# The first steps of a linear attention in an order written by hand on three engines

## The chip, the cores and the metric

The kernel runs on one core of a Trainium2 chip. The metric is the time on the device in microseconds (us), the median of several executions. A core has five engines that each work through an instruction stream of their own: TensorE (PE, the matmuls), VectorE (DVE), ScalarE (ACT), GpSimd (POOL) and SyncE (SP, here the issuer of plain transfers). They wait for one another by semaphores.

## The reference

Four images go through a small vision tower: a tokenizer, a first layer (attention over the images, then a mixture of six experts, two for each token), and a second layer (a linear attention, then four experts and a shared MLP). Only the join of the two layers and the linear attention matter here:

```
h   = h + combined                              # the two experts' rows of each token, weighted
x   = layernorm(h)
q, k, v = split(x @ W_qkv + b_qkv)
q, k = q - mean(q), k - mean(k)
q2, k2 = q*q, k*k
k2 = l2norm_over_tokens(k2 / (sum(k2) + 1e-7))  # a norm for each channel, over all tokens of the image
q2 = l2norm_over_channels(q2 / (sum(q2) + 1e-7))
kv = einsum('bnc,bnd->bcd', k2, v)
h   = h + (v + q2 @ kv / sqrt(N)) @ W_out + b_out
```

## The kernel before

**Tiles and units.** An image has 784 distinct tokens in seven tiles of 112 tokens. The linear attention works on *units* of four or three tiles: units 0 and 1 are image 0, units 2 and 3 are image 1, and so on up to unit 7. The residual stream `h` stays on chip.

**From the experts to the units.** The first layer's experts work in 30 blocks of 256 rows and write their rows to `yrows` in DRAM. When the last block is written, the rows of a unit come back by indirect gathers: `fetch(u)` (from L1352, the gather in L1361) has POOL issue two of them for each tile (one for each of a token's two experts) into a tile `ys`. Eight gathers make a unit of four tiles, six one of three. The pool of `ys` has three buffers (`bufs=3`), so a later unit's gathers wait until an earlier unit's rows have been read.

**Statistics.** `stats_one(u, j)` (from L1369) is DVE work on one tile: two multiply-adds `h += ys * wk` (L1375), one for each gathered row, each of which has to wait for its gather; then the layernorm's statistics (L1384, L1385). `normalise(u)` takes the root on ACT (L1394), the reciprocal (L1395) and writes the normalised rows `xa` (L1398); then `residual(u)` adds a bias row to `h` (L1409).

**Attention.** For each unit: `x_t` turns `xa` on PE; `q_k` (L1566 to L1575) makes q and k in PSUM (`pqk`), DVE adds the bias (L1570), ACT squares with running sums; `scales` (L1589 to L1603) makes the scale of each token and applies it on both engines, and squares the scaled k into `sq`; `fold` (L1610 to L1615) sums `sq` over the tiles on DVE; `q_t` turns q. For each image: `k_x` (from L1622) sums the squares over tokens on PE (`pn`), takes the norm `kn` (L1632 to L1634), multiplies k by x on PE (`pukx`, L1640) and scales the result into `g` (L1644). `g_t` turns `g`, `kv_out` multiplies it by `Wvo` and DVE finishes `kvo` (L1670), and `rows_out` (L1681, L1686) multiplies x and q into the output and adds it to `h` (L1692). `layer1_weights` makes `Wvo` and `bvo` once, from the weights.

**Who sets the order.** Some stretches of the program stand inside `tc.manual_schedule(engines=...)`: on the engines listed, their instructions keep the written order among themselves. Everything else is placed by a scheduler, which may also put it between the instructions of a hand-written stretch: in the program before, the two copies that make `bvs` in `layer1_weights` stand far ahead, between the first layer's attention steps. In the kernel before, the block loop of the experts is by hand on DVE and SP, and it also holds the statistics of units 0 and 1; all of the linear attention is left to the scheduler.

The loop of the linear attention goes over steps `u`. Step 0 fetches unit 3, turns unit 1 and makes `q_k`, `scales` and `fold` of unit 0; step 1 does the same for unit 1, with the weights in between. In step 1 `q_k` also makes the statistics of unit 2, tile by tile:

```
            if u:
                stats_one(u + 1, j)
```

Of the kernel before, what the change touches and what calls it, by code (L numbers as in the profile page):

```python
# [21 lines left out]
F32 = mybir.dt.float32  # L22
# [5 lines left out]
P = 128  # L28
TT = 112
NI = 4  # L30
TPI = 7
# [4 lines left out]
D = 256  # L36
# [24 lines left out]
def tile_vit_tower(ctx: ExitStack, tc: tile.TileContext, a: dict, out: bass.AP):  # L61
# [112 lines left out]
    def col(key, i=0, n=P):  # L174
        return cols[:n, rows[key] + i : rows[key] + i + 1]
# [415 lines left out]
        )  # L591

    def layer1_weights():
        WvT = w1p.tile([P, 2, D], F32, tag="WvT", name="WvT")
        pt = ps_tile("pwv").rearrange("p (k i) -> p k i", k=2)
        for k in range(2):
            for c in range(2):
                nc.tensor.transpose(
                    pt[:, k, c * P : (c + 1) * P],
                    Wqkv[:, c, 2 * D + k * P : 2 * D + (k + 1) * P], ident,  # L600
                )
        nc.vector.tensor_copy(WvT, pt)
        Wvo = w1p.tile([P, 2, D], F32, tag="Wvo", name="Wvo")
        for c in range(2):
            pw = ps_tile("pwvo")[:, :D]
            for k in range(2):
                nc.tensor.matmul(
                    pw, WvT[:, k, c * P : (c + 1) * P], Wout[:, k, :],
                    start=(k == 0), stop=(k == 1),
                )  # L610
            nc.scalar.copy(Wvo[:, c, :], pw)
        bvs = w1p.tile([P, 2, P], F32, tag="bvs", name="bvs")
        for k in range(2):
            nc.vector.tensor_copy(bvs[:, k, :], col("bv", k).to_broadcast([P, P]))
        bvo = w1p.tile([P, D], F32, tag="bvo", name="bvo")
        pw = ps_tile("pbvo")[:, :D]
        for k in range(2):
            nc.tensor.matmul(pw, bvs[:, k, :], Wout[:, k, :], start=(k == 0), stop=(k == 1))
        nc.vector.tensor_copy(bvo, pw)
        bres = bout  # L620
        nc.vector.tensor_tensor(bres, bout, bvo[:TT], ALU.add)
        return Wvo, bvo, bres

# [800 lines left out]
    with tc.manual_schedule(engines={mybir.EngineType.DVE, mybir.EngineType.SP}):  # L1426
        own_weights(NEARLY)
        turned(NEARLY)
        for i in range(NEARLY, NBLK + 1):
            if i < NBLK:  # L1430
                load(i + 3)
                hidden(i, 0)
            rows_back(i - 1)
            own_weights(i + 1)
            turned(i + 1)
            if i < NBLK:
                hidden(i, 1)
            if i == NEARLY + 1:
                centred_weights()
            for u in range(3):  # L1440
                if i - 1 == after[u]:
                    fetch(u)

            for u, wait, two in ((0, 4, 1), (1, 2, 2)):
                j = (i - 1 - after[u] - wait) * two
                for k in range(j, j + two):
                    if 0 <= k < units[u][2]:
                        stats_one(u, k)
                    elif k == units[u][2]:
                        normalise(u)  # L1450
            if i - 1 == after[0] + 10:
                x_t(0)
    layer0.close()


# [94 lines left out]
    def q_k(u, j0, j1):  # L1550

        n = units[u][2]
        xT = xTs[u]
        if j0 == 0:
            qks[u] = lin.tile([TT, GT, 2 * D], F32, tag="qk", name="qk")
            sumsof[u] = (
                small.tile([TT, GT, 2], F32, tag="ss", name="ss"),
                small.tile([TT, GT], F32, tag="s4", name="s4"),
            )
        qk = qks[u]  # L1560
        ss, s4 = sumsof[u]
        junk = lin.tile([TT, D], F32, tag="junk", name="junk", bufs=1)
        for j in range(j0, min(j1, n)):
            pqk = ps_tile("pqk")[:TT]
            for c in range(2):
                nc.tensor.matmul(  # L1566
                    pqk, xT[:, c, cut(j, 1)], Wqkv[:, c, : 2 * D],
                    start=(c == 0), stop=(c == 1),
                )
            nc.vector.tensor_tensor(qk[:, j, :], pqk, bqkv[:, : 2 * D], ALU.add)  # L1570

            for i in range(2):
                half = qk[:, j, i * D : (i + 1) * D]
                nc.scalar.activation(half, half, AF.Square, accum_out=ss[:, j, i : i + 1])  # L1574
            nc.scalar.activation(junk, qk[:, j, :D], AF.Square, accum_out=s4[:, j : j + 1])  # L1575
            if u:
                stats_one(u + 1, j)
        if j1 >= n and u:
            if u + 1 < len(units) and units[u + 1][2] > n:
                stats_one(u + 1, n)  # L1580
            normalise(u + 1)

    def scales(u):

        b, j0, n = units[u]
        qk = qks[u]
        ss, s4 = sumsof.pop(u)

        nc.vector.tensor_scalar(ss[:, :n], ss[:, :n], 1e-7, None, ALU.add)  # L1589
        nc.scalar.activation(s4[:, :n], s4[:, :n], AF.Sqrt, bias=zero[:TT])  # L1590
        nc.vector.scalar_tensor_tensor(
            ss[:, :n, 0], ss[:, :n, 0], 1e-12, s4[:, :n], ALU.mult, ALU.max
        )
        nc.vector.reciprocal(ss[:, :n], ss[:, :n])
        uk = uks[u] = lin.tile([TT, GT, D], F32, tag="uk", name="uk", bufs=3)
        sq = lin.tile([TT, GT, D], F32, tag="sq", name="sq", bufs=1)
        for j in range(n):
            nc.scalar.activation(uk[:, j, :], qk[:, j, D:], AF.Copy, scale=ss[:, j, 1:2])
            nc.vector.tensor_scalar(
                qk[:, j, :D], qk[:, j, :D], ss[:, j, 0:1], None, ALU.mult  # L1600
            )
        for j in range(n):
            nc.scalar.activation(sq[:, j, :], uk[:, j, :], AF.Square)  # L1603
        return sq

    def fold(u, sq):
        b, j0, n = units[u]
        if j0 == 0:
            acc = sums[b] = lin.tile([TT, 2, D], F32, tag="acc", name="acc")
            nc.vector.tensor_tensor(acc, sq[:, 0:2, :], sq[:, 2:4, :], ALU.add)  # L1610
        else:
            acc = sums[b]
            nc.vector.tensor_tensor(acc, acc, sq[:, 0:2, :], ALU.add)
            nc.vector.tensor_tensor(acc[:, 0, :], acc[:, 0, :], sq[:, 2, :], ALU.add)
            nc.vector.tensor_tensor(acc[:, 0, :], acc[:, 0, :], acc[:, 1, :], ALU.add)  # L1615
# [5 lines left out]

    def k_x(b):  # L1622

        acc = sums.pop(b)
        pn = psum_s.tile([P, 512], F32, tag="pss", name="pn")
        for c in range(2):
# [6 lines left out]
        nc.vector.tensor_scalar(kn, kn, 1e-12, None, ALU.max)  # L1633
        nc.vector.reciprocal(kn, kn)  # L1634
        g = gs[b] = lin.tile([P, 2, D + 2], F32, tag="g", name="g")
        for c in range(2):
            pg = ps_tile("pukx")[:, : D + 2]
            for j in range(TPI):
                u, k = (2 * b, j) if j < GT else (2 * b + 1, j - GT)
                nc.tensor.matmul(  # L1640
                    pg, uks[u][:, k, c * P : (c + 1) * P], xas[u % 4][:, k, : D + 2],
                    start=(j == 0), stop=(j == TPI - 1),
                )
            nc.vector.tensor_scalar(  # L1644
                g[:, c, :], pg, kn[:, c : c + 1], REP / math.sqrt(REP * SEQ),
                ALU.mult, ALU.mult,
            )
# [45 lines left out]

    squares = {}
    for u in range(len(units) + 2):
        b, odd = divmod(u - 2, 2)
        one_image = u >= 2 and not odd
        if u == 0:  # L1700
            fetch(3)
            x_t(1)
            q_k(0, 0, GT)
            squares[0] = scales(0)
            fold(0, squares.pop(0))
            continue
        if u < len(units):
            fetch(u + 3)
        if u == len(units):
            shared = shared1(0)  # L1710
        if one_image:
            k_x(b)
            q_t(u - 1)
        if u == 2:
            gT = g_t(0)
            kv_out(0, gT)
            rows_out(0)
            x_t(2)
        if u < len(units):
            q_k(u, 0, 2)  # L1720
        if one_image and b:
            gT = g_t(b)
        if u < len(units):
            q_k(u, 2, GT)
            if u == 1:
                lw.extend(layer1_weights())
                Wvo, bvo = lw[:2]
            squares[u] = scales(u)
        if one_image and b:
            kv_out(b, gT)  # L1730
        if u == len(units) - 1:
            rows_in(0)
            turn_rows(0)
            gate(0)
        if 2 <= u < len(units) - 1:
            x_t(u + 1)
        if u == 3:
            for k in range(3):
                residual(k)
        if u >= 2 and (b or odd):  # L1740
            rows_out(u - 2)
        if u < len(units):
            fold(u, squares.pop(u))
            if u % 2:
                q_t(u - 1)
    linear.close()
# [94 lines left out]
```

## Time and profile before

| | before |
|---|---|
| time, median of 3 | 816.67 us (815.66 to 820.11) |
| span of the profiled execution | 814.5 us |
| PE busy | 736.9 us, 90% of the span |
| DVE busy | 514.7 us, 63% |
| ACT busy | 318.5 us, 39% |
| POOL busy | 131.9 us, 16% |

The shares are means over stages that are limited by different things. The linear attention runs from about 506 us to 669 us, and the change lies in its first forty. For that stretch one needs the busy time of each engine in slices of ten microseconds, the timeline of DVE and POOL, and the chain of waits.

### The profile page before, as it was taken

How to read it: one execution, taken by the hardware profiler on the slowest of the kernel's cores; microseconds unless marked ns; L12 is line 12 of the kernel's file. 1: busy time of each engine (PE TensorE's matmuls, PEld its weight loads, DVE VectorE, ACT ScalarE, POOL GpSimd, SP SyncE). 2: the span in 40 equal slices, each digit the busy share in tenths (PEclk: the TensorE clock that was granted, in tenths of full speed). 3: DMA queues.
4: the chain of work that ended last, by engine and by line, in shares of the span. 5: the costliest groups of instructions: out<-in, count | busy, mean ns of one | idle time of the engine just before them, and what ended most of it. 6: DMA issues, size and time to landing. Idle time of an engine off the chain costs nothing. (4 is left out here: it accounts for less than half of the span.)

```text
span 814.5 us, 11185 instructions
## 1 busy us (share of the span) xinstructions
PE 736.9 (90%) x3669; PEld 520.4 (64%) x3669; DVE 514.7 (63%) x1619; ACT 318.5 (39%) x758; POOL 131.9 (16%) x151
## 2 busy tenths in 40 slices
PE   1879998899788887989999999699999999999996
PEld 1757785555555655878888887375776675555553
DVE  4477897486767985535545756699984745554441
ACT  0424434555376475333223322627544503222221
POOL 4200000000006450750013020676000000000000
PEclk9999999999999988999999999899999999999999
DMA  8999991000002167433234234322000002233323
GB/s 193 341 425 425 420 421 65 1 0 1 0 1 62 40 230 231 142 118 113 91 98 141 81 113 123 90 88 73 2 1 1 0 16 69 84 102 94 93 86 114
DMA packets 59182, 97.52 MB, mean 120 GB/s; under 512 B 15486, under 2 KB 49460, under 8 KB 54260
## 3 DMA queue, kind: packets, MB, share of 16 engines
q1 hardware_dynamic: 52700, 81.47, 28.7%
q0 software_dynamic: 6224, 14.13, 6.0%
q10 hardware_dynamic: 200, 1.21, 0.7%
q8 instruction: 29, 0.48, 0.2%
q14 instruction: 29, 0.24, 0.1%
HBM read 31.04 MB, written 65.74 MB: 119 GB/s over the span
## 5 line engine op out<-in xcount | busy, mean ns | idle before, releaser
L901 POOL DMA_INDIRECT xrows<-xn,pos x56 | 60.2, 1074 | 274.0 <-ACT kq L665 233.1
L1361 POOL DMA_INDIRECT ys<-yrows,pos x56 | 56.6, 1011 | 146.7 <-DMA yrows<-yb 130.6
L1168 PE MATMUL pb<-xTb,own 128*128 128x256 f32 x240 | 59.4, 392 | 3.8 <-DVE r L764 1.6
L1174 ACT ACTIVATE hb<-pb,own 128x256 f32<-128x256 f32 x74 | 35.0, 473 | 61.1 <-PE pb L1168 52.7
L1168 PE MATMUL pb<-hb,own 128*128 128x256 f32 x240 | 58.2, 385 | 0.3 <-DVE hb L1176 0.3
L1185 PE MATMUL pyb<-own,hb 128*128 128x256 f32 x240 | 56.9, 379 | 0.2 <-ACT hb L1174 0.2
L1168 PEld LDWEIGHTS pb<-xTb,own 128*128 128x128 f32 x240 | 45.4, 197 | 12.9 <-ACT hb L1174 1.9
L297 PE MATMUL pt<-ident,xn 112*128 112x112 f32 x280 | 42.3, 282 | 12.2 <-DVE xn L482 6.9
L1566 PE MATMUL pqk<-Wqkv,lxT 128*112 128x512 f32 x112 | 49.7, 594 | 0.5 <-ACT lxT L81 0.5
L1185 PEld LDWEIGHTS pyb<-own,hb 128*128 128x128 f32 x240 | 45.4, 190 | 6.8 <-ACT hb L1174 0.6
L297 PEld LDWEIGHTS pt<-ident,xn 112*128 112x128 f32 x280 | 32.6, 149 | 26.2 <-ACT xn L778 9.2
L1191 DVE TENSOR_TENSOR yb<-pyb,eb 128x512 f32<-128x512 f32 x30 | 20.7, 690 | 44.9 <-PE pyb L1185 44.5
L1168 PEld LDWEIGHTS pb<-hb,own 128*128 128x128 f32 x240 | 43.8, 192 | 6.2 <-DVE hb L1176 0.9
L306 PE MATMUL pe<-xT,eW 128*128 128x448 f32 x112 | 45.2, 546 | 0.0
L1158 ACT COPY xTb<-ptb 128x512 f32<-128x512 f32 x30 | 17.5, 583 | 62.7 <-PE ptb L1154 62.7
L1176 DVE TENSOR_SCALAR hb<-pb,own 128x256 f32<-128x256 f32 x46 | 22.1, 481 | 29.5 <-PE pb L1168 29.5
L317 PE MATMUL pwo<-Wo,oT 128*112 128x256 f32 x112 | 29.0, 412 | 7.5 <-DVE oT L730 6.7
L1566 PEld LDWEIGHTS pqk<-Wqkv,lxT 128*112 128x112 f32 x112 | 19.3, 177 | 24.8 <-issue 23.0
L690 DVE SCALAR_TENSOR_TENSOR prod<-kq 128x784 f32<-128x784 f32 x32 | 30.3, 969 | 7.3 <-ACT kq L665 5.0
L1574 ACT ACTIVATE qk<-qk 112x256 f32<-112x256 f32 x56 | 22.8, 407 | 28.5 <-DVE qk L1570 28.3
L306 PEld LDWEIGHTS pe<-xT,eW 128*128 128x128 f32 x112 | 20.2, 190 | 20.9 <-issue 20.7
L1145 DVE COPY own<-ew 128x1540 f32 x30 | 28.8, 963 | 3.9 <-DMA Wout<-in_L_attn_W_out_dram 1.1
(339 smaller groups left out, 1519.1 us busy)
## 6 DMA issues: line engine op xcount, KB each, us to landing
xrows<-nothing SPq DMA_DIRECT2D x19, 1024.0 KB
yrows<-nothing SPq DMA_DIRECT2D x19, 1024.0 KB
out_dram<-h SPq DMA_DIRECT2D x84, 112.0 KB
xb<-xrows SPq DMA_DIRECT2D x30, 256.0 KB
yrows<-yb SPq DMA_DIRECT2D x30, 256.0 KB
ew<-in_L_ffn_expert_w_dram SPq DMA_DIRECT2D x6, 768.0 KB
wb<-wd SPq DMA_DIRECT2D x28, 112.0 KB
img<-in_x_dram ACTq DMA_DIRECT2D x2, 588.0 KB
```

Of the source, the lines that this page charges most:

```text
L297: nc.tensor.transpose(pt[:, j * TT : (j + 1) * TT], xn[:, j, c * P : (c + 1) * P], ident[:TT, :TT])
L306: nc.tensor.matmul(pm[: wcols.stop - wcols.start, :n], w[:, c, wcols], xT(c), start=(c == 0), stop=(c == chunks - 1),)
L317: nc.tensor.matmul(pm[:, i, :], xT(c, t), w[:, c, :], start=(c == 0), stop=(c == chunks - 1))
L690: nc.vector.scalar_tensor_tensor(prod, qTs[s][:, o, :], 1.0, kT[:, o, t * SEQ : (t + 1) * SEQ], ALU.mult, ALU.mult, accum_out=atts[s][:, o ...
L901: put = nc.gpsimd.indirect_dma_start(out=xrows[:, :], out_offset=bass.IndirectOffsetOnAxis(ap=pos[:, k, t0 + j : t0 + j + 1], axis=0), in_ ...
L1145: nc.vector.tensor_copy(w, ewf[0][:, bass.ds(off, EW)])
L1168: nc.tensor.matmul(pm, wm[:, c, o * P : (o + 1) * P], src[:, c, :], start=(c == 0), stop=(c == 1),)
L1174: nc.scalar.activation(dst[:, o, :], pm, AF.Relu, bias=b)
L1185: nc.tensor.matmul(pm[:, t, :], src[:, c, t * P : (t + 1) * P], wm[:, c, :], start=(c == 0), stop=(c == 1),)
L1361: got = nc.gpsimd.indirect_dma_start(out=y[:, j, k, :], out_offset=None, in_=yrows[:, :], in_offset=bass.IndirectOffsetOnAxis(ap=pos[:, k, ...
L1566: nc.tensor.matmul(pqk, xT[:, c, cut(j, 1)], Wqkv[:, c, : 2 * D], start=(c == 0), stop=(c == 1),)
L1574: nc.scalar.activation(half, half, AF.Square, accum_out=ss[:, j, i : i + 1])
```

## The change

The first two steps of the loop are taken out of it and written out in a fixed order on DVE, PE and ACT: both units' `q_k` and `scales` first, then the folding of their squares, with unit 2's statistics tile by tile between the later steps. `fetch(3)` and `fetch(4)` now stand ahead of that stretch; before, `fetch(4)` stood in step 1. For this to be written, some functions are cut in two or moved:

- `scales` leaves the squares to a new `squares`, called later.
- `k_x` makes its products first and keeps both PSUM tiles; the norm of the sums moves to a new `k_norm`, for all images.
- `layer1_weights` is a generator in three pieces, and its `bvs` copies move ahead.
- `q_k` makes the next unit's statistics from unit 2 on, instead of unit 1.
- `x_t(1)` moves to the end of the block loop, and the bias of units 0 and 1 only (not 2) is added in step 3.

The aim is that the scales of two units, and with them k and q, are ready early, and that the third unit's statistics stand behind them.

```diff
@@ block loop
+            if i == NBLK:
+                x_t(1)
@@ q_k
-            if u:
+            if u > 1:
                 stats_one(u + 1, j)
-        if j1 >= n and u:
+        if j1 >= n and u > 1:
...
             normalise(u + 1)
@@ scales
-        for j in range(n):
-            nc.scalar.activation(sq[:, j, :], uk[:, j, :], AF.Square)
-        return sq
+    def squares(u):
+        sq = sqs[u] = lin.tile([TT, GT, D], F32, tag="sq", name="sq", bufs=1)
+        for j in range(units[u][2]):
+            nc.scalar.activation(sq[:, j, :], uks[u][:, j, :], AF.Square)
@@ k_x: products first, the norm of the sums in k_norm
...
@@ the loop's first two steps
-    squares = {}
-    for u in range(len(units) + 2):
...
-        if u == 0:
-            fetch(3)
-            x_t(1)
-            q_k(0, 0, GT)
-            squares[0] = scales(0)
-            fold(0, squares.pop(0))
-            continue
+    pgs = {}
+    fetch(3)
+    fetch(4)
+    with tc.manual_schedule(engines=by_hand):
+        q_k(0, 0, GT)
+        q_k(1, 0, 2)
+        scales(0)
+        weights = layer1_weights()
+        q_k(1, 2, GT)
+        next(weights)
+        scales(1)
+        next(weights)
+        q_t(0)
+        squares(0)
+        fold(0)
+        squares(1)
+        stats_one(2, 0)
+        stats_one(2, 1)
+        next(weights)
+        fold(1)
+        k_x(0)
+        stats_one(2, 2)
+        k_norm(0)
+        q_t(1)
+        stats_one(2, 3)
+        Wvo, bvo = lw[:2]
+        gT = g_t(0)
+        normalise(2)
+        kv_out(0, gT)
+        rows_out(0)
+        x_t(2)
+    for u in range(2, len(units) + 2):
```

More of the change, by code (lines that the diff above doesn't have):

```diff
@@ L602, in layer1_weights @@
         nc.vector.tensor_copy(WvT, pt)
+        bvs = w1p.tile([P, 2, P], F32, tag="bvs", name="bvs")
+        for k in range(2):
+            nc.vector.tensor_copy(bvs[:, k, :], col("bv", k).to_broadcast([P, P]))
+        yield
         Wvo = w1p.tile([P, 2, D], F32, tag="Wvo", name="Wvo")
@@ L611, in layer1_weights @@
             nc.scalar.copy(Wvo[:, c, :], pw)
[L612 to L615, printed above, removed]
         pw = ps_tile("pbvo")[:, :D]
@@ L618, in layer1_weights @@
             nc.tensor.matmul(pw, bvs[:, k, :], Wout[:, k, :], start=(k == 0), stop=(k == 1))
+        yield
+        bvo = w1p.tile([P, D], F32, tag="bvo", name="bvo")
         nc.vector.tensor_copy(bvo, pw)
@@ L621, in layer1_weights @@
         nc.vector.tensor_tensor(bres, bout, bvo[:TT], ALU.add)
-        return Wvo, bvo, bres
+        lw.extend((Wvo, bvo, bres))
+        yield
     scale = REP / math.sqrt(CHEAD) / math.sqrt(REP * SEQ)
@@ L1595, in scales @@
         uk = uks[u] = lin.tile([TT, GT, D], F32, tag="uk", name="uk", bufs=3)
-        sq = lin.tile([TT, GT, D], F32, tag="sq", name="sq", bufs=1)
         for j in range(n):
@@ L1601, in scales, with fold @@
             )
-        for j in range(n):
-            nc.scalar.activation(sq[:, j, :], uk[:, j, :], AF.Square)
-        return sq
-    def fold(u, sq):
+    def squares(u):
+        sq = sqs[u] = lin.tile([TT, GT, D], F32, tag="sq", name="sq", bufs=1)
+        for j in range(units[u][2]):
+            nc.scalar.activation(sq[:, j, :], uks[u][:, j, :], AF.Square)
+    sqs = {}
+    def fold(u):
+        sq = sqs.pop(u)
         b, j0, n = units[u]
@@ L1622, in k_x, with k_norm @@
     def k_x(b):
+        pgs[b] = []
+        for c in range(2):
+            pg = ps_tile("pukx")[:, : D + 2]
+            for j in range(TPI):
+                u, k = (2 * b, j) if j < GT else (2 * b + 1, j - GT)
+                nc.tensor.matmul(
+                    pg, uks[u][:, k, c * P : (c + 1) * P], xas[u % 4][:, k, : D + 2],
+                    start=(j == 0), stop=(j == TPI - 1),
+                )
+            pgs[b].append(pg)
+    def k_norm(b):
         acc = sums.pop(b)
@@ L1635, in k_x @@
         g = gs[b] = lin.tile([P, 2, D + 2], F32, tag="g", name="g")
[L1636 to L1643, printed above, removed]
+        for c, pg in enumerate(pgs.pop(b)):
             nc.vector.tensor_scalar(
@@ L1692, in rows_out @@
             nc.vector.tensor_tensor(ht, pm[:, : len(two), :], ht, ALU.add)
-    squares = {}
-    for u in range(len(units) + 2):
-        b, odd = divmod(u - 2, 2)
-        one_image = u >= 2 and not odd
-        if u == 0:
-            fetch(3)
-            x_t(1)
-            q_k(0, 0, GT)
-            squares[0] = scales(0)
-            fold(0, squares.pop(0))
-            continue
+    pgs = {}
[30 more added lines that the diff above has]
+    for u in range(2, len(units) + 2):
+        b, odd = divmod(u - 2, 2)
+        one_image = not odd
         if u < len(units):
@@ L1710, in tile_vit_tower @@
             shared = shared1(0)
-        if one_image:
+        if one_image and b:
             k_x(b)
+            k_norm(b)
             q_t(u - 1)
[L1714 to L1718, printed above, removed]
         if u < len(units):
@@ L1724, in tile_vit_tower @@
             q_k(u, 2, GT)
[L1725 to L1728, printed above, removed]
+            scales(u)
+            squares(u)
         if one_image and b:
@@ L1734, in tile_vit_tower @@
             gate(0)
-        if 2 <= u < len(units) - 1:
+        if u < len(units) - 1:
             x_t(u + 1)
         if u == 3:
-            for k in range(3):
+            for k in range(2):
                 residual(k)
-        if u >= 2 and (b or odd):
+        if b or odd:
             rows_out(u - 2)
         if u < len(units):
-            fold(u, squares.pop(u))
+            fold(u)
             if u % 2:
```

## The prediction

> **What bounds the kernel now.** I read the busy time in slices of 10 us first, to find which engine limits which part of the linear attention:
>
> ```profile
> 510.00:520.00 10.00, 9.04 (x25) 3.72 (x23) 5.50 (x14) 4.75 (x22) 6.83 (x8) 1.00 0.24 70
> 520.00:530.00 10.00, 4.40 (x10) 3.53 (x11) 8.56 (x27) 7.59 (x30) 7.56 (x9) 0.69 0.31 93
> ...
> 560.00:570.00 10.00, 10.00 (x44) 6.71 (x43) 9.96 (x33) 8.23 (x32) 4.24 (x5) 1.00 0.22 64
> 570.00:580.00 10.00, 10.00 (x51) 7.70 (x50) 9.73 (x30) 3.01 (x9) 0.00 (x0) 1.00 0.01 2
> ```
>
> The columns are the slice, then PE, PEld, DVE, ACT and POOL busy, the clock that PE was granted, and DMA. PE idles 5.6 us in 520 to 530, with its clock down to 0.69 for part of it. From 550 on it never rests: 89.5 of 90 us to 640. So PE bounds everything after 550, and a delay of PE before that cannot be won back. The chain of waits shows how PE enters that stretch:
>
> ```profile
> 538.63 0.89 DVE g L1644 x2
> ...
> 540.78 1.99 PE pkvo L1666 x8
> ...
> 543.64 0.86 PE pout L1686 x4
> ```
>
> DVE finishes `g` of image 0 at 539.5, PE makes `pkvo`, DVE makes `kvo`, and at 543.64 PE starts the first product with `kvo` (L1686). This is the clock I use: when does this product start in the changed program?
>
> The timelines of DVE and POOL show what DVE waits for early on:
>
> ```profile
> 513.67 0.48 DVE L1375 SCALAR_TENSOR_TENSOR h<-ys,wk,h 112x256 f32<-112x256 f32 x1 [2.92 <-DMA ys<-yrows,pos]
> 514.07 0.68 DVE L1570 TENSOR_TENSOR qk<-pqk,bqkv 112x512 f32<-112x512 f32 x1
> ```
> ```profile
> 511.04 0.92 POOL L1361 DMA_INDIRECT ys<-yrows,pos  x1 [21.73 <-DMA yrows<-yb]
> 512.26 0.93 POOL L1361 DMA_INDIRECT ys<-yrows,pos  x1 [0.30 <-issue]
> ...
> 520.87 0.99 POOL L1361 DMA_INDIRECT ys<-yrows,pos  x1 [0.30 <-DVE h L1375]
> ...
> 528.70 0.92 POOL L1361 DMA_INDIRECT ys<-yrows,pos  x1 [0.30 <-DVE xa L1398]
> ...
> 538.73 0.92 POOL L1361 DMA_INDIRECT ys<-yrows,pos  x1 [0.30 <-DVE xa L1398]
> ...
> 546.81 0.92 POOL L1361 DMA_INDIRECT ys<-yrows,pos  x1 [0.30 <-issue]
> ...
> 552.22 1.37 POOL L1361 DMA_INDIRECT ys<-yrows,pos  x1 [0.30 <-issue]
> ```
>
> POOL issues the gathers of units 2 to 7 without a rest from 511.04, about 1.23 us apart: unit 2 (eight), unit 3 from 520.87 (six), unit 4 from 528.70 (eight), unit 5 from 538.73, unit 6 from 546.81; 552.22 is the fifth of unit 6. The view of the tile `ys` gives the landing after the issue:
>
> ```profile
> DMA to landing us min/median/max: 2.6/2.7/3.3
> ```
>
> And DVE obeys its order. PE made `pqk` tiles every 1.74 us (12.18 us for seven), the third by about 511.7; its addition ran at 514.07, because a multiply-add that waited 2.92 us for a gather stood ahead of it.
>
> [...]the gathers here take 0.92 to 1.44 us, so the pace has a floor of 1.23 us and may stretch. [...]here `pwvo` (eight matmuls) took 3.78 us after 6.56 us idle, against 1.99 us for `pkvo`, equally large.
>
> **The change part by part.** PE's order stays up to `pukx`; ACT's and DVE's do not. The decisive part does not stand in the diff but in the order of the changed program's DVE instructions. Unit 2's statistics are now fixed behind `fold(0)`. The statistics of units 3 to 6 are outside the block, and the scheduler has put their multiply-adds *into* it, each with its wait for its gather, ahead of what the block was written for. In order, with units read from the operands:
>
> ```
> qk unit 0 (4), qk unit 1 tile 0
> ys unit 3: three; qk unit 1 tile 1; ys unit 3: three
> ys unit 4: two, and between them the scales of unit 0; ys unit 4: one
> qk unit 1 tile 2, WvT, bvs; ys unit 4: four, and between them the scales of unit 1
> ys unit 4: one; ys unit 5: six; ys unit 6: one; lqT; ys unit 6: two; fold(0)
> ys unit 2 (landed) and ys unit 6 (fourth, fifth), in turn
> statistics of units 2 to 6, bvo, fold(1), residual(1); kn, g; ...; kvo
> ```
>
> So before `g` DVE waits for the fifth gather of unit 6, the 33rd of the train. Before, what stood ahead of `g` needed only gathers issued by about 535. The new wait's queue holds unit 1's q and k, both units' scales, `WvT` (for which PE waits), `fold` (for which `pn` waits), `g` and `kvo`.
>
> *The wait.* Gather 33 was issued at 552.22. At the floor it would be 511.04 + 32 x 1.227 = 550.3; POOL's buffers come free in time either way (unit 5 now takes unit 3's, whose last gather lands about 530). With 2.7 us to land: 553.0 to 555.5; I take 554.0[...]. Up to there each gather comes 1.2 us after the last and DVE has less than that to do between, so the arrival sets the time. The matmuls behind `WvT` (about 537) and the scales of unit 1 (about 540) are done long before.
>
> *From there to the end of `g`* (spacing from start to start in DVE's timeline): 5 multiply-adds x 0.39 = 1.95; 14 statistics x 0.33 = 4.6; 10 aggregates x 0.09 = 0.9; `bvo` and `bres` 0.7; `fold(1)` 0.60 + 0.33 + 0.33 = 1.26; residual(1) 0.84; `kn` twice 0.3; `g` twice 0.79. Sum 11.3 us. `pn` and `kn`'s root fit inside: the sums are complete at 6.8 us, the root took 1.3 us after them before, and `kn` is due at 9.6.
>
> *From `g` to the end of `kvo`:* `lqT` 0.41, 5 multiply-adds 1.95, 3 statistics 1.0, aggregate 0.1, 3 reciprocals 0.36, 5 `xa` x 0.31 = 1.55, residual(2) 1.12, `kvo` 0.8: 7.3 us. PE needs 3.3 us from `g` to the end of `pkvo` (539.5 to 542.8)[...]: hidden beside this.
>
> So `kvo` ends at 554.0 + 11.3 + 7.3 = 572.6, where it ended at 543.30: L1686 starts **29.0 us** later than at 543.64.
>
> *The clock.* PE will have idled from about 550 in pieces. `pwvo` and `pbvo` lost 2.45 us to the low clock before (3.57 + 1.57 from start to start, against 1.83 + 0.86). The output products lose between 0 and 2.5; I take 1.2.
>
> *Later images.* The norm now follows the products. For images 1 and 2, 3.4 us of `pqk` hide it. For the last, only `lqT`'s transposes (0.57) and `pws` (0.1) stand between, against some 1.6 us from `pn` to the end of `g` (root 0.26, `kn` 0.35, `g` 0.87, hops): 0.9 us.
>
> *What it saves.* The 7 us of PE idle before `pwvo` lie in front of the same wait and are worth nothing. DVE will be lighter after 573, since units 3 to 6 have been added already, but PE is full there: nothing. The split of `scales`, the moved `bvs`, `x_t(1)` and the residual move hidden work: nothing.
>
> Sum: 29.0 + 1.2 + 0.9 = 31.1, so 816.67 + 31.1 = 847.8, rounded to **848 us**.
>
> **The rivals.** *(a) The hoisted waits are cheap.* The written order then does what it is for, PE's idle before `pwvo` shrinks, and 816.7 - 7 = about 810 us. For it: DVE had 4.5 of 10 us free in 510 to 520. Against: POOL's gathers are issued at a fixed pace, and DVE let `qk` wait for one. Slower is missed only if the stream is not run as built; the trace of before follows its own built order exactly. *(b) About the same:* the delay is taken up later. Against it: PE is busy 89.5 of 90 us after 550. 817 us. *(c) A smaller delay:* gathers at the floor, DVE's run of small instructions faster (18.6 us becomes 15) and no clock loss: 816.7 + 553.0 - 554.0 + 29.0 - 3.6 + 0.9 = 842 us or a little under. *(d) A larger one:* [...](1.44 us for each gather would put the 33rd 5 us later) and the full clock loss: 848 + 5 + 1.3 + some waits after `kvo` (unit 6's and 7's last multiply-adds stand there too) = 854 to 858 us.
>
> **How the numbers follow.** The forecast (843 to 852) 0.70; (c) 0.11; (d) 0.13; (a) 0.04; (b) 0.02. The range takes in most of (c) and (d): 839 to 855. Faster by over 0.5% 0.04, within 0.5% 0.02, slower 0.94.
>
> **What would show it.** Right: DVE waits for gathers 15 to 20 times between 520 and 557, with waits of about 1 us; the fifth multiply-add of unit 6 near 554; `g` near 565, `kvo` near 572; PE busy under half of 520 to 570, and full after. POOL's train keeps its pace. Wrong: `g` before 550, or PE resting after 575, or the gathers themselves moving.

## The result and the profile after

The changed kernel takes **845.24 us** (843.52 to 848.91) beside 818.72 us (815.66 to 821.21) for the kernel before, measured together: ratio 1.0332, 95% interval 1.0297 to 1.0367, so 3.3% slower. The forecast was 848, the range 839 to 855. In the two profiles the span grew from 814.5 to 842.7 us, by 28.2 us.

The busy time in slices of 10 us, with the columns of the prediction (slice; PE, PEld, DVE, ACT, POOL busy; clock granted to PE; DMA):

```profile
510.00:520.00 10.00, 9.43 (x25) 3.86 (x23) 2.76 (x4) 5.99 (x28) 7.04 (x8) 1.00 0.26 74
520.00:530.00 10.00, 0.00 (x0) 0.00 (x0) 3.51 (x8) 1.49 (x7) 7.56 (x9) 0.71 0.33 96
...
550.00:560.00 10.00, 0.25 (x2) 0.25 (x2) 9.25 (x31) 1.03 (x3) 7.58 (x8) 0.58 0.30 86
560.00:570.00 10.00, 7.48 (x26) 5.49 (x26) 10.00 (x33) 1.96 (x6) 2.44 (x3) 0.57 0.15 43
...
580.00:590.00 10.00, 9.76 (x28) 4.29 (x27) 9.73 (x31) 7.09 (x31) 0.00 (x0) 1.00 0.00 0
```

PE does nothing at all from 520 to 530, where it was busy for 4.40 us before, and 0.25 us from 550 to 560, where it was busy for 9.52. From 580 on it is all but full again (9.76). What was lost was lost between 520 and 571.

DVE's timeline has the multiply-adds of `h`, `g` and `kvo` (the start, the duration of the group, what it waited for in brackets); POOL's has the first gather of the train and the last ahead of `g`; the view of the tile `ys` sums up who waited for it (us, times):

```profile
523.33 0.48 DVE L1379 SCALAR_TENSOR_TENSOR h<-ys,wk,h 112x256 f32<-112x256 f32 x1 [7.04 <-DMA ys<-yrows,pos]
...
553.02 0.48 DVE L1379 SCALAR_TENSOR_TENSOR h<-ys,wk,h 112x256 f32<-112x256 f32 x1 [0.19 <-DMA ys<-yrows,pos]
...
563.18 0.86 DVE L1660 TENSOR_SCALAR g<-pukx,kn 128x258 f32<-128x258 f32 x2
...
570.35 0.86 DVE L1686 SCALAR_TENSOR_TENSOR kvo<-bvo,g,pkvo 128x256 f32<-128x256 f32 x2
```
```profile
510.82 0.92 POOL L1365 DMA_INDIRECT ys<-yrows,pos  x1 [21.12 <-DMA yrows<-yb]
...
550.29 0.92 POOL L1365 DMA_INDIRECT ys<-yrows,pos  x1 [0.30 <-issue]
```
```profile
  DVE h L1379: 19.2, 18
...
DMA to landing us min/median/max: 2.6/2.7/3.9
```

POOL's second line here is the 33rd gather, issued at 550.29: 32 steps of 1.23 us after the first. It lands 2.7 us later, and at 553.02 the multiply-add that waited for it starts. `g` ends at 564.04 and `kvo` at 571.21. In all, DVE's multiply-adds waited 18 times, 19.2 us. The first wait, 7.04 us, is the longest: it is for unit 3's first gather, the ninth of the train. Unit 2's eight go ahead of it on POOL, but DVE adds them only after 550. The chain that ended last now runs through DVE where it ran through PE's `pkvo` before:

```profile
570.43 0.40 DVE kvo L1686
...
570.88 1.12 PE pout L1702 x4
```

And PE, whose waits name what it needed each time, first in the kernel before, then in the changed one:

```profile
525.60 3.78 PE L607 MATMUL pwvo<-Wout,WvT 128*128 128x256 f32 x8 [6.56 <-DVE WvT L602]
...
543.48 1.03 PE L1686 MATMUL pout<-kvo,lqT 128*112 128x256 f32 x4
```
```profile
536.01 3.78 PE L612 MATMUL pwvo<-Wout,WvT 128*128 128x256 f32 x8 [16.58 <-DVE WvT L603]
...
559.75 1.02 PE L1650 MATMUL pn<-ones,acc 112*128 112x1 f32 x4 [11.41 <-DVE acc L1625]
...
570.88 1.12 PE L1702 MATMUL pout<-kvo,lqT 128*112 128x256 f32 x4 [0.92 <-DVE kvo L1686]
```

It waited 16.58 us for `WvT` (6.56 before), 11.41 for the sums `acc`, and 0.92 for `kvo`. The product with `kvo` starts at 570.88 instead of 543.48. (The chain of waits puts the start in the kernel before at 543.64; from here on the timeline's 543.48 is used.)

### The profile page after: what moved, and what is told of

The parts are those of the page before. It is cut to its first block, busy times and chain, and to the rows that moved or that the text cites. A ratio compares the mean times of both kernels' runs of the same rounds, so it can differ in the third digit from the quotient of the medians.

```text
span 842.7 us, 11182 instructions
## 1 busy us (share of the span) xinstructions
PE 740.4 (88%) x3669; PEld 522.7 (62%) x3669; DVE 516.8 (61%) x1619; ACT 319.1 (38%) x758; POOL 129.5 (15%) x151
## 3 DMA queue, kind: packets, MB, share of 16 engines
q1 hardware_dynamic: 52700, 81.47, 28.2%
## 5 line engine op out<-in xcount | busy, mean ns | idle before, releaser
L1365 POOL DMA_INDIRECT ys<-yrows,pos x56 | 54.4, 972 | 146.1 <-DMA yrows<-yb 130.0
L1172 PE MATMUL pb<-hb,own 128*128 128x256 f32 x240 | 58.1, 385 | 0.3 <-DVE hb L1180 0.3
L1379 DVE SCALAR_TENSOR_TENSOR h<-ys,wk,h 112x256 f32<-112x256 f32 x56 | 26.2, 475 | 19.4 <-DMA ys<-yrows,pos 19.2
L1580 ACT ACTIVATE qk<-qk 112x256 f32<-112x256 f32 x56 | 22.8, 408 | 33.7 <-DVE qk L1576 33.7
```

The costliest lines, as they stand in the source:

```text
L1172: nc.tensor.matmul(pm, wm[:, c, o * P : (o + 1) * P], src[:, c, :], start=(c == 0), stop=(c == 1),)
L1365: got = nc.gpsimd.indirect_dma_start(out=y[:, j, k, :], out_offset=None, in_=yrows[:, :], in_offset=bass.IndirectOffsetOnAxis(ap=pos[:, k, ...
L1379: nc.vector.scalar_tensor_tensor(h[:, t, :], ys[u][:, j, k, :], wk[:, k, t : t + 1], h[:, t, :], ALU.mult, ALU.add,)
```

## The experiments

The forecast came out, but that does not prove its reasons. **Theory A**: the scheduler put the multiply-adds of units 3 to 6 into DVE's hand-written stretch, each with its wait for a gather, and what the stretch is for had to wait behind them. The rivals say that the time went elsewhere: to the hand-written order on PE and ACT, to the norms that now follow the products, or to the amount of DVE's work in the stretch.

Two numbers are read from each profile: **lead**, from the start of the first `pqk` product to the start of the first output product with `kvo`, and **tail**, from there to the end of the span.

| kernel | start of pqk | product with kvo | lead | tail | span | median (ratio to before, interval) |
|---|---|---|---|---|---|---|
| before | 506.42 | 543.48 | 37.1 | 271.0 | 814.5 | 818.72 |
| changed | 506.81 | 570.88 | 64.1 | 271.8 | 842.7 | 845.24 (1.0332, 1.0297 to 1.0367) |
| units 3 and up barred | 510.11 | 547.64 | 37.5 | 283.9 | 831.5 | 833.45 (1.0202, 1.0153 to 1.0251) |
| units 4 and up barred | 509.09 | 560.44 | 51.4 | 281.4 | 841.8 | 842.12 (1.0314, 1.026 to 1.0369) |
| units 5 and up barred | 506.31 | 561.54 | 55.2 | 271.7 | 833.2 | 836.8 (1.0272, 1.0218 to 1.0325) |
| before, norm after the products | 509.48 | 548.52 | 39.0 | 273.2 | 821.7 | 821.93 (1.0058, 1.0038 to 1.0079) |
| changed, DVE free | 506.06 | 548.17 | 42.1 | 273.4 | 821.6 | 824.3 (1.0095, 1.0068 to 1.0122) |
| before, WvT early | 507.44 | 545.25 | 37.8 | 271.0 | 816.2 | 817.57 (0.9998, 0.9973 to 1.0023) |

The start of `pqk` differs by up to 4 us between the profiles, and by 3.1 us even between the kernel before and the one with the norm after the products, whose code is the same up to there. So leads, tails and places counted from the first `pqk` are compared, and not places in the span.

Six more runs, in two jobs, stand apart. The kernel before took about 5% longer there (854.16 and 859.06 us), and the profiles of all six show long waits that nothing in the program releases, so their numbers are not compared with those of the table.

### Bars ahead of the later units

In three kernels the multiply-adds of the later units read a copy of the gather weights `wk` which DVE makes as the last step of the hand-written stretch. They cannot be placed before it. With N = 2, 3, 4 the bar holds units 3, 4 or 5 and all above:

```
+    wks = [wk]
-                h[:, t, :], ys[u][:, j, k, :], wk[:, k, t : t + 1], h[:, t, :],
+                h[:, t, :], ys[u][:, j, k, :], wks[u > N][:, k, t : t + 1], h[:, t, :],
...
         x_t(2)
+        wk2 = lina.tile([TT, 2, NT], F32, tag="wk2", name="wk2", bufs=1)
+        nc.vector.tensor_copy(wk2, wk)
+        wks.append(wk2)
```

All of units 3 and up barred:

> The changed kernel, but the multiply-adds of units 3 to 7 read a copy of the weights that DVE makes at the end of the hand-written stretch, so the scheduler cannot put them inside it. Theory (waits for hoisted gathers): DVE waits for no gather of unit 3 or later before kvo; the first product with kvo (L1686 of the kernel before) starts near 540 us instead of 570.9, and the time is 812 to 818 us. Rival A (the written order itself is slow: two units' scales and the weights ahead of everything): still 838 us or more. Rival B (the norm after the products, in all images, costs most of it): still 838 us or more.

Measured 833.45 us: the time is a miss, and the product starts at 547.64 instead of near 540. Of the span, 3.3 us more than in the changed kernel lie ahead of `pqk`. PE's timeline:

```profile
525.89 1.99 PE L612 MATMUL pwvo<-Wout,WvT 128*128 128x256 f32 x8 [3.17 <-DVE WvT L603]
...
547.64 1.29 PE L1703 MATMUL pout<-kvo,lqT 128*112 128x256 f32 x4
...
565.91 1.42 PE L297 MATMUL pt<-ident,xa 112*128 112x112 f32 x6 [3.66 <-DVE xa L1403]
...
578.36 0.42 PE L297 MATMUL pt<-ident,xa 112*128 112x112 f32 x2 [3.22 <-DVE xa L1403]
```

PE waits 3.17 us for `WvT` instead of 16.58, and the lead is back to 37.5 us, 0.4 more than in the kernel before. So it was the later units' work in the stretch that made it 64.1. But the tail grew by 12.1 us over the changed kernel's: two new waits for `xa`, 3.66 and 3.22 us, and a low clock behind them (0.76 and 0.84 from 560 to 580). The statistics of units 3 and 4 now all come after the stretch, and POOL's timeline shows what else they hold:

```profile
562.11 0.92 POOL L1365 DMA_INDIRECT ys<-yrows,pos  x1 [11.65 <-DVE h L1380]
```

The tile `ys` has three buffers. Until unit 3's rows are read, unit 6's gathers cannot start: POOL rests 11.65 us for DVE's `h`. A bar takes one wait away and makes another.

Units 4 and up barred:

> As the run before, but only units 4 to 7 are barred; unit 3's six multiply-adds stay hoisted. Theory: DVE is held until the 14th gather of the train lands, near 529.5; with the chain behind it worked out by hand from there the first product with kvo starts near 554, and the time is about 829 us. Rival C (it is the hoisted work, not its waits): six multiply-adds and their statistics are some 4 us of DVE time, so 4 us over the run with all barred, about 819.

Units 5 and up barred:

> Only units 5 to 7 barred; units 3 and 4 stay hoisted, 14 multiply-adds. Theory: held until the 22nd gather lands, near 539.4; the first product with kvo near 559, the time about 834 us. Rival C: some 10 us of DVE work over the run with all barred, about 825.

Measured 842.12 and 836.8 us. The second is near its expectation (836.8 beside 834), the first is a miss by 13 us; rival C's smaller values (819, 825) are missed by both. The leads are the safer measure: rival C adds 4 and 10 us to the 37.5 with all barred, and measured are 13.8 and 17.7 more. PE of the first, and DVE of the second around `WvT`:

```profile
535.96 3.78 PE L612 MATMUL pwvo<-Wout,WvT 128*128 128x256 f32 x8 [14.25 <-DVE WvT L603]
...
560.44 1.13 PE L1703 MATMUL pout<-kvo,lqT 128*112 128x256 f32 x4
...
586.25 1.98 PE L297 MATMUL pt<-ident,xa 112*128 112x112 f32 x8 [5.15 <-DVE xa L1403]
```
```profile
532.61 0.48 DVE L1380 SCALAR_TENSOR_TENSOR h<-ys,wk,h 112x256 f32<-112x256 f32 x1 [0.51 <-DMA ys<-yrows,pos]
...
534.75 0.68 DVE L603 COPY WvT<-pwv 128x512 f32<-128x512 f32 x1
```

Taking units 5 and 6 away from the queue shortens the lead from 64.1 to 55.2 us, taking unit 4 away too only to 51.4, and taking unit 3 away to 37.5. The reason shows when `pwvo` is counted from the first `pqk`. It starts 29.2 us behind it in the changed kernel and also with units 5 and up barred: in both, `WvT` stands behind the 17th gather, unit 4's third. With units 4 and up barred it stands behind the 14th, unit 3's last, and `pwvo` starts after 26.9 us; with all barred after 15.8. Behind the start of `pwvo`, PE takes 34.9 us to the product in the changed kernel, and 24.5 and 26.1 in the two with the later bars. The wait for `WvT` was there all along, in front of the longer one.

The step from all barred to unit 3 let in also tells waiting from work. Six multiply-adds and three statistics are some 4 us of DVE's time by the expectation, and they made the lead 13.8 us longer; DVE waited 10.8 us for their six gathers. And with unit 4 barred the tail pays as with all barred: 5.15 us for unit 4's `xa`.

### DVE's order left to the scheduler

The reverse test keeps every instruction, PE's order and ACT's hand-written stretch, and lets the scheduler order DVE:

```
-    with tc.manual_schedule(engines=by_hand):
+    with tc.manual_schedule(engines=by_hand - {ENG.DVE}):
```

> The changed kernel with VectorE's order left to the scheduler and TensorE's and ScalarE's by hand as they are, once more: the one difference to the changed kernel is where the same instructions stand in VectorE's queue. Theory: the 27 us come back but for what the norms after the products cost; TensorE waits about 5 us for WvT (16.58 in the changed kernel) and under 2 us for acc (11.41), first product with kvo 40 to 44 us after the first pqk (64.1), time 818 to 826. Rival B (the order by hand on TensorE and ScalarE costs most): 55 us or more, time 835 or more. If waits without a releaser in the program fill the stretch again, the run is no answer to either.

Measured 824.3 us, in the range of the theory, as are the lead and the wait for `WvT`; the wait for `acc` is longer than the 2 us expected. Rival B is refuted. PE's timeline:

```profile
523.80 3.51 PE L612 MATMUL pwvo<-Wout,WvT 128*128 128x256 f32 x8 [5.13 <-DVE WvT L603]
...
538.07 1.01 PE L1650 MATMUL pn<-ones,acc 112*128 112x1 f32 x4 [2.99 <-DVE acc L1625]
...
548.17 1.03 PE L1702 MATMUL pout<-kvo,lqT 128*112 128x256 f32 x4
```

The wait for `WvT` is 5.13 us and that for `acc` 2.99, and the lead is 42.1 us. The scheduler placed unit 2's multiply-adds first, and ahead of `g` only such later ones as had their rows by then or nearly so. Of the changed kernel's 64.1 us, 22.0 are thus due to the places of the same instructions on one engine. Against the kernel before 5.0 us of lead and 2.4 of tail remain.

### The norm after the products, alone

The kernel before with nothing but the split, for all images: `k_x` keeps the products, and `k_norm` behind it makes the sums over tokens, `kn` and `g`, as in the change:

```
             k_x(b)
+            k_norm(b)
             q_t(u - 1)
```

> The kernel before with one part of the change: in every image the products of k and x come first and the norm of the sums after them. Theory: only the last image feels it, by about 0.9 us (the first perhaps by as much): 819 to 820.5 us where the kernel before has 818.7. Rival B: 825 us or more.

Measured 821.93 us, by the medians 5.8 more than the kernel before had in that job (816.17): above the theory's values and below rival B's. In the profile 2.0 us are in the lead and 2.2 in the tail. The last image's norm in three profiles, the kernel before, the kernel with the split, the changed kernel:

```profile
654.70 1.99 PE L1666 MATMUL pkvo<-Wvo,gT 128*128 128x256 f32 x8 [0.58 <-ACT gT L1657]
```
```profile
658.67 0.94 PE L1660 MATMUL pgT<-ident,g 128*128 128x128 f32 x4 [0.62 <-DVE g L1650]
660.29 3.57 PE L1672 MATMUL pkvo<-Wvo,gT 128*128 128x256 f32 x8 [0.68 <-ACT gT L1663]
```
```profile
681.11 0.94 PE L1670 MATMUL pgT<-ident,g 128*128 128x128 f32 x4 [0.62 <-DVE g L1660]
682.73 1.99 PE L1682 MATMUL pkvo<-Wvo,gT 128*128 128x256 f32 x8 [0.67 <-ACT gT L1673]
```

From the transposes of q ahead of these lines to `pkvo`, PE takes 12.30 us in the kernel before and 13.35 in both others: the split costs 1.05 us for the last image by itself. PE waits 0.62 and 0.68 us in one, 0.62 and 0.67 in the other. But the eight `pkvo` matmuls that follow take 3.57 us in the first and 1.99 in the second. All six kernels of the table with the split have these two waits. With DVE free `pkvo` takes 3.68 us and with units 4 and up barred 3.58; with the other two bars it takes 1.99. So up to 1.7 us come on top where the granted clock drops: it was 0.83 over the 10 us that hold `pkvo` in these three profiles, and 1.00 in the other three. With one profile of each, it is not known whether this belongs to the kernel or to the execution. The last image (2.7 us) and the 2.0 us of the first are over half of the 8.5 us by which the kernel with DVE free stays behind the kernel before; the rest was not taken apart.

### The transposes early, alone

Could the purpose of the change be had without the order by hand? The kernel before, with `layer1_weights` cut after the copy `WvT` and its first part written ahead of `q_k(0, 0, GT)`:

```
         nc.vector.tensor_copy(WvT, pt)
+        yield
...
             x_t(1)
+            weights = layer1_weights()
+            next(weights)
             q_k(0, 0, GT)
...
-                lw.extend(layer1_weights())
+                next(weights)
```

> The kernel before with the four transposes of Wqkv and the copy WvT written ahead of the first unit's q_k, and nothing else of the change, once more. Theory: the 6.56 us that TensorE waited for WvT go, 2 to 5 us of them are kept, first product with kvo 32 to 36 us after the first pqk (37.1 in the kernel before), time 811 to 815. Rival E (the scales and the gathers set the stage anyway): TensorE waits about as long before pt of qk or pukx, time within 1.5 us of the kernel before.

Measured 817.57 us, ratio 0.9998: rival E. PE's timeline:

```profile
519.45 1.89 PE L608 MATMUL pwvo<-Wout,WvT 128*128 128x256 f32 x8
...
531.08 4.54 PE L1642 MATMUL pukx<-xa,uk 112*128 112x258 f32 x12 [3.83 <-ACT uk L1600]
...
538.33 1.30 PE L1656 MATMUL pgT<-ident,g 128*128 128x128 f32 x4 [1.78 <-DVE g L1646]
540.30 3.78 PE L1668 MATMUL pkvo<-Wvo,gT 128*128 128x256 f32 x8 [0.67 <-ACT gT L1659]
```

`pwvo` starts at 519.45 with no wait, at a granted clock of 1.00 (510 to 530). But PE now waits 3.83 us for the scaled k of unit 1 in the middle of `pukx`, and 1.78 for `g`; behind them the granted clock is down (0.75 from 540 to 550), and `pkvo` takes 3.78 us, where it took 1.99. Unit 1's scales, on DVE, had not come forward as far as PE's work had: counted from the first `pqk`, their reciprocal moved from 25.6 to 22.8 us and `pwvo` from 19.2 to 12.0. The 6.56 us before `pwvo` in the kernel before hid the next waits; they were not there to be won by feeding PE alone.

### The six runs that stand apart

Two of the six have edits shown above (DVE free, the transposes early). The others are the change with no order by hand (twice), with half the gathers, and with two bars:

```
no order by hand     -    with tc.manual_schedule(engines=by_hand):
                     +    with ExitStack():
half the gathers     -            for k in range(2):                     (in fetch)
                     +            for k in range(1):
                     -    ys[u][:, j, k, :]   +    ys[u][:, j, 0, :]     (in stats_one)
two bars             a copy of wk for units 3 and 4 right after scales(1),
                     another for units 5 and up at the end of the stretch
```

> The changed kernel with the order by hand kept on TensorE and ScalarE, and VectorE's order left to the scheduler; the instructions are the same. In its VectorE order the copy WvT now stands behind unit 2's eighth gather instead of unit 4's third (the 17th), and g behind the 21st gather instead of the 33rd. Theory (the place of the later units' multiply-adds in VectorE's queue costs the time): WvT near 524, first product with kvo near 547 (570.88 in the changed kernel), time 818 to 825. Rival B (TensorE's fixed order, or the norms after the image's products, costs most): product past 556, time 835 or more.

> The changed kernel without any order by hand: the statements stand as the change wrote them and the scheduler orders all three engines. TensorE's order comes out the same as in the changed kernel; VectorE's g stands behind the twelfth gather. Theory: first product with kvo at 543 to 548, time 816 to 824, close to the kernel before plus what the norms after the products cost (5.8 us in the run of that part alone). Rival B: as TensorE's order is the same, the time stays at 835 or more.

> The changed kernel with one gather for each tile instead of two: the second multiply-add of a tile reads the same gathered rows, so every gather of the second expert's rows is left out, and nothing of VectorE's work. WvT stands behind the tenth gather instead of the 17th and g behind the 18th instead of the 33rd. From the train of the changed kernel (first at 510.82, one each 1.23 us, 2.7 to landing) the tenth lands at 524.6 and the 18th at 534.4, 18 us before the 33rd did. Theory (the gathers in the queue set it): first product with kvo near 552, time 823 to 831. Rival C (VectorE's own work in the stretch sets it, the gathers only happen to be there): product past 564, time 838 or more.

> The changed kernel with two bars instead of one: units 3 and 4 read a copy of the gather weights that VectorE makes just after the second unit's scales, units 5 and later one that it makes at the end of the order by hand. So no multiply-add of a later unit can stand before WvT and the two scales, and those of units 3 and 4 may fill VectorE's waits behind them. Theory: WvT near 522, g near 545, first product with kvo at 546 to 551, and less of the waits for xa that the bar on all units brought at 562 and 575; time 819 to 826. Rival D (a bar only moves the wait: units 5 and 6 come late and TensorE waits for their xa): waits for xa of over 4 us in all after 560, time 830 or more.

> The same kernel as in the run of the written order without the order by hand, once more[...]. Theory: first product with kvo 37 to 42 us after the first pqk (37.1 in the kernel before, 64.1 in the changed one), time 816 to 824. Rival B (TensorE's order, which is that of the changed kernel, sets the time): more than 55 us, 835 or more.

> The kernel before with one part of the change's purpose alone, and no order by hand: Wqkv's four transposes and the copy WvT are written ahead of the first unit's q_k instead of after the second's. The 6.56 us that TensorE waited for WvT before the product pwvo go, as WvT is there when pqk ends at 518.9. Theory: TensorE then needs unit 0's lqT and unit 1's scales next, which stood ready 1 to 5 us ahead; 2 to 5 us are kept, first product with kvo at 539 to 542, time 811 to 815. Rival E (the scales and the gathers set the stage anyway): a wait before pt of qk or before pukx takes the place of the one removed, time within 1.5 us of the kernel before.

| kernel | lead | median | ratio to before in the same job (interval) |
|---|---|---|---|
| DVE free | 59.1 | 855.44 | 1.0032 (1.001 to 1.0053) |
| no order by hand | 58.1 | 856.12 | 1.001 (0.9988 to 1.0033) |
| half the gathers | 50.9 | 844.03 | 0.9882 (0.9846 to 0.9918) |
| two bars | 57.2 | 853.52 | 0.9985 (0.9964 to 1.0007) |
| no order by hand, again | 58.2 | 861.1 | 1.003 (0.999 to 1.0071) |
| transposes early | 62.6 | 857.88 | 0.9982 (0.9946 to 1.0018) |

All the times that the theory expected are missed. The times fall where the rivals put them, but in these jobs the kernel before itself, at 854 us and more, passes the rivals' 835 too. DVE's timeline of the first run shows why:

```profile
565.96 0.42 DVE L622 COPY bvo<-pbvo 128x256 f32<-128x256 f32 x1 [18.47 <-remote]
```

DVE rests 18.47 us before a copy, and its releaser is "remote": nothing in the program that the profile shows. PE then rests 19.2 us for ACT, which waits for DVE. Waits of this kind, of 8 us and more, stand in all six leads, released by "remote" or "issue" (no releaser seen). The orders differ, and but for one the leads hardly do: these ratios say nothing of the order. One reading survives: in no order by hand and two bars the long waits come behind `pwvo`, and it starts 16.6 us (in both runs) and 15.6 us behind the first `pqk`, beside 29.2 in the changed kernel. With the later multiply-adds out of its way, `WvT` was early there too. That half the gathers gave the shortest lead agrees with theory A, but as its lead too has such a wait (8.32 us of PE ahead of `pwvo`), it is no proof. The changed kernel itself was not run in these jobs. DVE free and the transposes early were repeated later, as told above; no order by hand, half the gathers and two bars have no undisturbed run, and what they were to tell of the whole lead stays open.

## Why the prediction was right

**The deciding wait: right.** 554.0 was forecast for the multiply-add of the 33rd gather, 553.02 measured. The train kept the floor of 1.23 us; the 1 us allowed for a slower pace, my own estimate, was not needed. The waits came as told, 18 of them, though not all near 1 us: the first took 7.04, the others 0.7 on average.

**From there to `kvo`: right.** 11.3 us to the end of `g`, measured 11.0 (553.02 to 564.04); 7.3 to the end of `kvo`, measured 7.2 (564.04 to 571.21). The sum of spacings of small instructions from the kernel before held to about 2%. The product needs only the first half of `kvo`: it starts 0.3 us before `kvo`'s end, where it started 0.2 us behind it in the kernel before. So it moved by 27.4 us and `kvo` by 27.9, where 29.0 was forecast.

**The clock: too large.** 1.2 us were set for slow output products. The first four took 1.12 us, against 1.03 before, and the next 1.03, at a granted clock of 1.00 from 569 on: 0.1 us. The low clock (0.50 from 560 to 567, `pkvo` 3.42 us) fell on work that was waiting anyway: `pkvo` ended at 569.09, and DVE came to `kvo` at 570.35.

**The last image: right here.** 0.9 forecast; from the transposes of q to `pkvo` PE lost 1.05, and the whole tail grew by 0.8 us. But the run of the split alone, whose tail grew by 2.2 us, shows that this term can be larger: the range did not count a drop of the clock there (0.66 granted from 660 to 665).

**"Worth nothing": right as a sum, too simple as a reason.** PE's wait for `WvT` grew to 16.58 us and cost nothing, since the wait for `acc` and `g` came behind it. The bars show that it is a second bound close behind the first: with units 5 and 6 out of the way `pwvo` starts as late as in the changed kernel, and the lead is still 55.2 us.

The sum, 31.1 us, compares with 28.2 of the spans and 26.5 of the medians measured together; against the median that the prediction started from, 816.67, it is 28.6. So the sum was 3 to 5 us too large, and that 848 lies as near as 2.8 us to 845.24 is in part luck: the kernel before, measured again, was 2.05 us slower than the number that the sum was added to. The cause is confirmed from both sides: with the later units' multiply-adds out of the stretch the lead is 37.5 us, and with the same instructions in another order on DVE alone 42.1, against 64.1. How much of the whole is waiting and how much the later units' statistics themselves was not separated by a run, as both stand or fall with the place of the multiply-adds, and the run with half the gathers gave no clear answer. For unit 3 alone the bars show mostly waiting (13.8 us of lead for some 4 us of work). The changed kernel's profile has 19.2 us of waits up to 553.02 and 18.2 us of DVE work behind it, that of the stretch itself included.

Rival (a), that the hoisted waits are cheap, falls with the 18 waits and PE's empty slices; (b) with the tail, which gives nothing back in any kernel of the table; (d) with the pace of the gathers. Its delay was also worked out wrongly: 1.44 us is the length of one slow gather, and with the 0.30 us before the next the pace would be 1.74, which puts the 33rd some 16 us behind the floor and not 5. (c) named the right pace and no clock loss, and took DVE's run for shorter than it was.

## What to carry to other kernels

Fixing an order by hand does not keep a scheduler from putting other work between an engine's instructions, and DVE took what it was given in turn: in the changed kernel `pqk` was done at 518.99, and its last addition but one ran at 526.32, behind multiply-adds that had waited 7.04, 0.79 and 0.82 us. So read the built order, and for every instruction that waits for a transfer ask what stands behind it. Fix only what the stretch needs and leave room: a bar against the late work took 26.5 us off the lead, and gave 12.1 back where that work was then due and its buffers were held. A wait that is removed is worth only its distance to the next one: 6.56 us without `WvT` came to nothing, since the scales stood close behind.

## What the runs showed of the hardware

The same two short waits of PE ahead of the last image's `pkvo`, 0.62 and 0.67 or 0.68 us, were followed by a granted clock of 1.00 over the next 5 us in the changed kernel (682 to 687) and of 0.66 in the kernel with the split alone (660 to 665); `pkvo` took 1.99 and 3.57 us. In three of six profiles with these waits it was slow, 3.57 to 3.68 us. No run shows what decides between the two.

In the two jobs that stand apart engines rested without a releaser that the profile shows in the program: DVE for 18.47 us in the first run, PE for 15.20 and ACT for 11.44 in the two with no order by hand. No view shows what held them.
